# A graph network in four layers: edge weights moved to ScalarE and run counts cut in halves

## The chip, the cores and the metric

The kernel runs on one core of one Trainium2 chip. Times are device microseconds of one execution, from the start to the end of the program on that core. TensorE (PE) multiplies matrices; its weight loads (PEld) are shown apart, since they overlap its multiplications. VectorE (DVE) and ScalarE (ACT) work elementwise, GpSimd (POOL) issues the indirect gathers here, and SyncE (SP) issues plain DMAs.

## The reference

A graph of 3125 nodes with 256 features and 50,000 edges, sorted by their destination, goes through four layers. Each layer adds a graph network and a mixer to the nodes, and then a feed-forward part. The change touches layer 1's graph network only, two hypergraph convolutions in a row:

```python
def _hconv(x, src, dst, ew, w1, b1, w2, b2, g, b):
    h = jax.nn.relu(x @ w1 + b1)
    msg = ew[:, None] * h[src]
    agg = jax.ops.segment_sum(msg, dst, num_segments=x.shape[0])
    h = agg @ w2 + b2
    return jax.nn.relu(_bn(h, g, b))
...
h = _hconv(x, src, dst, hyperedge_weight, c1_w1, c1_b1, c1_w2, c1_b2, c1_g, c1_b)
h = jax.nn.relu(_bn(h, bn1_g, bn1_b))
h = _hconv(h, src, dst, hyperedge_weight, c2_w1, c2_b1, c2_w2, c2_b2, c2_g, c2_b)
h = _bn(h, bn2_g, bn2_b)
return jax.nn.relu(h + residual)
```

Layer 3's graph network has three convolutions over the same edges without weights. The kernel does them with a dense matrix that holds how many edges lead from each node to each other, and it builds that matrix while layer 1 runs.

## The kernel before

Nodes are padded to 25 blocks of 128 (`NB`). The edges are padded to 416 slots of 128 edges (`NS`), so that all edges of one slot have their destination in the same block. For each slot, `self.src` holds the 128 source rows, `self.dl` the destination within the block, `self.ew` the weight, and `self.blk` the block's number.

`gather_sum` is the loop over edges. It takes the slots in groups of four (`G`), 104 groups in all. For each slot of a group, POOL issues an indirect DMA (L531) that fetches 128 rows of 256 features from a table in DRAM into a part of the tile `msg`; the tile holds a group, and there are seven of them. DVE then makes, for each slot, a 128x128 one-hot `oh` of the destinations. With `weighted=True`, which layer 1 alone uses, the entry is the edge's weight in place of one, and each slot has its own `tensor_scalar` (L566); without it, `one_hot` makes four with one `tensor_tensor` (L538). TensorE multiplies each one-hot with the slot's messages into PSUM (`g`, L585; each fp32 multiplication is two instructions in the trace). DVE adds the four results of the group before to `agg` at the block's place, which it reads from `self.blk` at run time (L527, L544).

Layer 1 runs this loop twice, once per convolution. In `layer1`, `loop` hands `gather_sum` a generator `both`, from which it takes one step after each group. A step advances two other pieces of work: `mix1`, layer 1's mixer (59 steps, all within the first loop), and `more`, which is different work in each loop:

- In the first, `sorted_edges` sorts the edges of every run of 16 slots by source block into `self.rooms`, in 78 steps: eight of preparation, then ten rounds of seven. A round has one-hots of the source blocks (`ohk`), a scan, four products, and four one-hots `ohr` of 2048 columns (L2041).
- In the second, `counts` goes over the 40 runs (`NR`), two steps each. A run makes two one-hots for its 25 places, `ohs` and `ohd` (L2065, 128x3200 each, one buffer each). TensorE multiplies them place by place (L2078), four to a PSUM tile, after it has added the result of the run before, `last`, times `on` where the run goes on in the same block (L2076). ACT copies the PSUM tiles to `T` as bf16 (L2080; two buffers). Then DVE adds an identity to one block of `T` (L2088), ACT looks for counts too large to be exact (`junk`, L2091), and SP writes `T` to `self.counted` in DRAM (L2092).

The columns' numbers 0 to 127 lie in SBUF as `self.cols`. Layer 1 has a PSUM tile `sums` of three parts: the first is the accumulator of `mix1` (shown as `acc`), the second a copy of `self.cols`, the third the same plus one. `sorted_edges` and `counts` read the second and third.

The program states waits by the tiles that instructions read and write. A scheduler puts the instructions of each engine into an order when the program is built, so that instructions of the loop, the mixer and `more` are mixed on every engine; on the chip each engine keeps that order. Each gather waits for the matmuls that read its `msg` tile seven groups before.

Of the kernel before, what the change touches and what calls it, by code (L numbers as in the profile page):

```python
# [9 lines left out]
F32 = mybir.dt.float32  # L10
BF16 = mybir.dt.bfloat16
# [8 lines left out]
P = 128  # L20
# [10 lines left out]
G = 4  # L31
# [18 lines left out]
def bc(ap, shape):  # L50

    idx, full = [], []
    own = list(ap.shape)
    for n in shape:
        if n is None:
            idx.append(slice(None))
            full.append(own.pop(0))
        else:
            idx.append(None)
            full.append(n)  # L60
    assert not own
    return ap[tuple(idx)].to_broadcast(full)


class Net:
# [466 lines left out]
            out=out, out_offset=None, in_=table,  # L532
            in_offset=bass.IndirectOffsetOnAxis(ap=self.src[:, t:t + 1], axis=0))

    def one_hot(self, pool, g):

        oh = pool.tile([P, G, P], F32, name="oh")
        self.nc.vector.tensor_tensor(oh, bc(self.dl[:, g * G:(g + 1) * G], [None, None, P]),  # L538
                                     bc(self.cols, [None, G, None]), ALU.is_equal)
        return oh  # L540

    def add_to(self, agg, t, q, w):
# [4 lines left out]
        for j in range(G):  # L547
            self.add_to(agg, g * G + j, q[j], agg.shape[2])

    def gather_sum(self, pool, ps, table, w, agg, weighted=False, steps=None):  # L550

        nc = self.nc
        sums = {}
        n = 1024 // w
        for g in range(NS // G):
            msg = []
            for j in range(G):
                if j % n == 0:
                    m = pool.tile([P, n, w], F32, name="msg", bufs=7)
                self.gather(m[:, j % n, :], table, g * G + j)  # L560
                msg.append(m[:, j % n, :])
            if weighted:
                oh = pool.tile([P, G, P], F32, name="oh", bufs=3)
                for j in range(G):
                    t = g * G + j
                    nc.vector.tensor_scalar(oh[:, j, :], self.cols, self.dl[:, t:t + 1], self.ew[:, t:t + 1],  # L566
                                            op0=ALU.is_equal, op1=ALU.mult)
            else:
                oh = self.one_hot(pool, g)
            if g:  # L570
                self.add_group(agg, g - 1, sums.pop(g - 1))
            sums[g] = self.sum_group(ps, oh, msg, w)
            if steps is not None:
                next(steps, None)
        self.add_group(agg, g, sums.pop(g))
# [1089 lines left out]
    def layer1(self):  # L1665
        nc, tc = self.nc, self.tc
        self.norm_x()
        with self.pool("rooms", 1) as c, self.pool("gnn", 1) as gw, self.pool("gnn2", 2) as gp, \
                self.pool("mix", 1) as mw, self.pool("mix2", 2) as mp, \
                self.pool("ps1", 3, PSUM) as ps, ExitStack() as own:  # L1670
            pool = Pools(gw, gp, CONV_ONE)

            sums = ps.tile([P, 3, P], F32, name="acc0", bufs=1)
            nc.scalar.copy(sums[:, 1, :], self.cols)
            nc.vector.tensor_scalar(sums[:, 2, :], self.cols, 1.0, None, op0=ALU.add)
            steps = self.mix1(mw, mp, ps, sums[:, 0, :])

            def loop(tab, agg, more):
                def both():
                    for _ in range(NS // G):  # L1680
                        next(steps, None)
                        next(more, None)
                        yield

                self.gather_sum(pool, ps, tab, D, agg, weighted=True, steps=both())
                for _ in more:
                    pass


            self.rooms = c.tile([P, NR, 2 * NB], BF16, name="rooms")  # L1690
            self.run_blk = c.tile([1, NR], I32, name="run_blk")
            self.goes_on, self.begins = (c.tile([P, NR], F32, name=n) for n in ("goes_on", "begins"))

            self.unfit = c.tile([P, 3], F32, name="unfit")

            tab, agg, *rest = self.conv_head(pool, ps, 1, self.xT)
            with self.pool("sort", 1, side="right") as bp:
                with ExitStack() as inner:
                    loop(tab, agg, self.sorted_edges(bp, ps, inner, sums[:, 1, :]))
            with self.pool("res", 1, side="right") as hp:  # L1700
                hT = hp.tile([P, 2, NP], F32, name="hT")
                self.conv_tail(pool, ps, agg, *rest, hT)
                sc, sh = self.batch_norm(pool, hT, self.plain(gw, "L1_gnn_bn1_g"), self.plain(gw, "L1_gnn_bn1_b"), "bn")
                self.relu_of(hT, sc, sh)
                tab, agg, *rest = self.conv_head(pool, ps, 2, hT)
            with self.pool("count", 1, side="right") as bp:
                loop(tab, agg, self.counts(bp, ps, sums[:, 1:, :]))
            hp = own.enter_context(self.pool("res", 1, side="right"))
            hT = hp.tile([P, 2, NP], F32, name="hT")
            self.conv_tail(pool, ps, agg, *rest, hT)  # L1710
            for _ in steps:
                pass
            sc, sh = self.batch_norm(pool, hT, self.plain(gw, "L1_gnn_bn2_g"), self.plain(gw, "L1_gnn_bn2_b"), "bn")
            for s, n in SUPER:
                for k in range(2):
                    h = hT[:, k, s:s + n]
                    nc.vector.scalar_tensor_tensor(h, h, sc[:, k:k + 1], self.xT[:, k, s:s + n], op0=ALU.mult,
                                                   op1=ALU.add)
                    nc.scalar.activation(h, h, AF.Relu, bias=sh[:, k:k + 1])
                for t in range(s // P, (s + n) // P):  # L1720
                    q = ps.tile([P, 512], F32, name="mm")[:, :D]
                    for k in range(2):
                        nc.tensor.transpose(q[:, k * P:(k + 1) * P], hT[:, k, t * P:(t + 1) * P], self.ident)
                    self.add_x(t, q)
# [326 lines left out]
    def counts(self, p, ps, cols):  # L2051
# [6 lines left out]
        over = p.tile([P, NR, 2], F32, name="over")  # L2058
        nc.vector.memset(over, 0.0)
        last = None  # L2060
        for u in range(NR):
            oh = []
            for k, name in enumerate(("ohs", "ohd")):
                t = p.tile([P, NB, P], BF16, name=name)
                nc.vector.tensor_tensor(t, bc(self.rooms[:, u, k * NB:(k + 1) * NB], [None, None, P]),  # L2065
                                        bc(cols[:, 1 - k, :], [None, NB, None]), ALU.is_equal)
                oh.append(t)
            on = p.tile([P, P], BF16, name="on", bufs=2)
            nc.scalar.mul(on, ident, self.goes_on[:, u:u + 1])
            yield  # L2070
            T = p.tile([P, NB, P], BF16, name="T", bufs=2)
            for k0 in range(0, NB, 4):
                n = min(4, NB - k0)
                q = ps.tile([P, 512], F32, name="mm")[:, :n * P]
                if last is not None:
                    nc.tensor.matmul(q, on, last[:, k0:k0 + n, :], start=True, stop=False)  # L2076
                for k in range(n):
                    nc.tensor.matmul(q[:, k * P:(k + 1) * P], oh[0][:, k0 + k, :], oh[1][:, k0 + k, :],  # L2078
                                     start=last is None, stop=last is None or k == n - 1)
                nc.scalar.copy(T[:, k0:k0 + n, :], q.rearrange("p (k d) -> p k d", d=P))  # L2080
                if k0 == 12:
                    yield

            Tf = T.rearrange("p k d -> p (k d)")
            r = nc.values_load(self.run_blk[0:1, u:u + 1], engines=(ET.DVE, ET.SP), min_val=0, max_val=NB - 1,
                               skip_runtime_bounds_check_because=IN_RANGE)
            own = Tf[:, bass.ds(r * P, P)]
            nc.vector.scalar_tensor_tensor(own, ident, self.begins[:, u:u + 1], own, op0=ALU.mult, op1=ALU.add)  # L2088
            for i, k0, k1 in ((0, 0, 13), (1, 13, NB)):
                junk = p.tile([P, 13 * P], BF16, name="junk")[:, :(k1 - k0) * P]  # L2090
                nc.scalar.activation(junk, Tf[:, k0 * P:k1 * P], AF.Relu, bias=full, accum_out=over[:, u, i:i + 1])  # L2091
            nc.sync.dma_start(self.counted[bass.ds(r * P, P), :], Tf)  # L2092
            last = T
        nc.vector.tensor_reduce(self.unfit[:, 1:2], over.rearrange("p u i -> p (u i)"), axis=AX.X, op=ALU.max)
        nc.vector.tensor_scalar(self.unfit[:, 1:2], self.unfit[:, 1:2], 0.0, None, op0=ALU.is_gt)
        one = p.tile([P, 1], F32, name="one")
# [313 lines left out]
```

## Time and profile before

| | |
|---|---|
| median of 3 runs | 6230.42 us (6222.06 to 6235.17) |
| the profiled execution | 6871.84 us, span 6870.1 us |
| instructions | 81944 |
| busy: PE, PEld, DVE | 4752.5, 3363.4, 3279.0 us |
| busy: ACT, POOL | 1573.9, 2383.8 us |
| granted TensorE clock, mean | 0.825 |
| loop 1, first gather to last add | 683 us |
| loop 2, first gather to last add | 808 us |
| layer 1's gathers (L531) | 832, 820.0 us busy, 986 ns each |
| weighted one-hots (L566) | 832, median 340 ns each |
| adds to `agg` (L544), all layers | 1664, 697.1 us busy |
| `ohs`, `ohd` (L2065) | 40 each, medians 3486 and 3479 ns |
| copies to `T` (L2080) | 280, median 586 ns |

The profile is of one execution, and that execution was 641 us longer than the median of the runs without it. Busy time of an engine is the sum of its instructions' durations; on DVE and ACT neighbours overlap a little, so that they can start closer together than they last. "Idle before, with a releaser" names the instruction whose end let a waiting one start. "Remote" and "another core or an unknown queue" are stalls for which the profile found no releaser.

### The profile page before, as it was taken

How to read it: one execution, taken by the hardware profiler on the slowest of the kernel's cores; microseconds unless marked ns; L12 is line 12 of the kernel's file. 1: busy time of each engine (PE TensorE's matmuls, PEld its weight loads, DVE VectorE, ACT ScalarE, POOL GpSimd, SP SyncE). 2: the span in 40 equal slices, each digit the busy share in tenths (PEclk: the TensorE clock that was granted, in tenths of full speed). 3: DMA queues.
4: the chain of work that ended last, by engine and by line, in shares of the span. 5: the costliest groups of instructions: out<-in, count | busy, mean ns of one | idle time of the engine just before them, and what ended most of it. 6: DMA issues, size and time to landing. Idle time of an engine off the chain costs nothing.

```text
span 6870.1 us, 81944 instructions
## 1 busy us (share of the span) xinstructions
PE 4752.5 (69%) x25310; PEld 3363.4 (49%) x25310; DVE 3279.0 (48%) x8628; ACT 1573.9 (23%) x4113; POOL 2383.8 (35%) x2340
## 2 busy tenths in 40 slices
PE   2375776396575556555577756777169999997797
PEld 1012344284454434433366313444046788786696
DVE  5146676634687537775534346667533200113222
ACT  1012223322100034442222112221124311101222
POOL 1605776321665534445231625665110000001211
PEclk9677888598787777777688877888589999997898
DMA  3362333264222223333155322333111232123454
GB/s 106 85 179 66 107 107 102 83 199 118 86 84 74 71 76 116 116 109 102 53 167 173 90 79 83 102 107 94 37 55 62 72 135 87 58 78 113 171 175 160
DMA packets 385094, 710.59 MB, mean 103 GB/s; under 512 B 100817, under 2 KB 223256, under 8 KB 384652
## 3 DMA queue, kind: packets, MB, share of 16 engines
q1 hardware_dynamic: 266431, 425.79, 20.0%
q0 software_dynamic: 108064, 269.63, 13.6%
q10 hardware_dynamic: 10157, 9.80, 0.4%
q8 instruction: 213, 3.49, 0.2%
q14 instruction: 229, 1.88, 0.1%
HBM read 571.51 MB, written 133.47 MB: 103 GB/s over the span
## 4 chain that ended last, share of the span: by engine, by line
PE 46%; issue 17%; DVE 15%; another core or an unknown queue 8%; DMA 5%; POOL 4%; ACT 3%; DVEq 2%; ACTq 1%; SPq 0%; POOLq 0%
PE dn L2134 12%; PE mm L465 6%; PE g L862 5%; PE g L585 3%; DVE agg L544 3%; PE y L1507 3%; PE h L1494 2%; DVE ohd L2065 2%; PE q L657 1%; PE q L666 1%; DMA terms<-outr 1%; PE mm L502 1%; DVEq L527 1%; PE mm L2194 1%
## 5 line engine op out<-in xcount | busy, mean ns | idle before, releaser
L531 POOL DMA_INDIRECT msg<-L_gnn_c_tab,src x832 | 820.0, 986 | 857.4 <-PE g L585 236.2
L531 POOL DMA_INDIRECT msg<-L_gnn_htab,src x832 | 893.7, 1074 | 588.6 <-issue 225.2
L544 DVE TENSOR_TENSOR agg<-agg,g 128x256 f32 (+2 forms) x1664 | 697.1, 419 | 588.6 <-remote 283.5
L2134 PEld LDWEIGHTS <-a 128*128 128x128 bf16 x7500 | 735.0, 98 | 118.1 <-issue 30.2
L862 PE MATMUL g<-msg,oh 128*128 128x261 f32 (+1 forms) x1664 | 591.8, 463 | 248.7 <-DVE agg L544 114.2
L585 PE MATMUL g<-msg,oh 128*128 128x256 f32 x1664 | 565.9, 489 | 229.0 <-DVE oh L566 138.7
L862 PEld LDWEIGHTS g<-msg,oh 128*128 128x128 f32 x1664 | 324.0, 218 | 510.3 <-issue 213.7
L585 PEld LDWEIGHTS g<-msg,oh 128*128 128x128 f32 x1664 | 387.7, 249 | 345.9 <-DVE oh L566 156.4
L1494 PE MATMUL h<-xe,w 128*128 128x128 f32 x3584 | 435.6, 278 | 7.3 <-DMA w<-in_L_ffn_W 7.3
L2134 PE MATMUL dn<-ha,a 128*128 128x256 bf16 x3750 | 426.2, 274 | 9.3 <-ACT ha L2119 7.8
L1511 POOL DMA_INDIRECT back<-y,toi x168 | 163.2, 971 | 773.4 <-DVE y L1510 537.9
L1507 PE MATMUL y<-w,hT 128*128 x1792 | 431.2, 388 | 0.0
L1494 PEld LDWEIGHTS h<-xe,w 128*128 128x128 f32 x3584 | 421.1, 194 | 8.7 <-issue 8.3
L2134 PE MATMUL dn<-hb,a 128*128 128x256 bf16 x3750 | 413.6, 273 | 0.0
L1498 ACT ACTIVATE hT<-h,br 128x128 f32<-128x128 f32 x896 | 256.3, 369 | 661.0 <-issue 572.7
L1418 POOL IOTA sl<- 1x56 f32 x3 | 0.5, 171 | 1123.7 <-PE dn L2134 1023.8
L1507 PEld LDWEIGHTS y<-w,hT 128*128 128x128 f32 x1792 | 326.5, 190 | 57.0
L1510 DVE COPY y<-y 128x256 f32<-128x256 f32 x168 | 71.2, 424 | 574.6 <-PE y L1507 574.4
L819 ACT COPY stage<-dm 128x24 bf16 (+1 forms) x832 | 182.7, 221 | 578.9 <-PE pd L825 193.5
L657 PE MATMUL q<-ohl,t 128*104 128x512 bf16 (+1 forms) x702 | 204.1, 423 | 126.3 <-issue 69.7
L1389 POOL DMA_INDIRECT sent<-xs,ids x150 | 154.8, 1032 | 355.9 <-DVE run L1368 189.2
L531 POOL DMA_INDIRECT ase<-tab,src x208 | 219.1, 1054 | 151.7 <-PE q L657 85.7
(724 smaller groups left out, 7619.8 us busy)
## 6 DMA issues: line engine op xcount, KB each, us to landing
a<-counted SPq DMA_DIRECT2D x100, 800.0 KB
w<-in_L_ffn_W SPq DMA_DIRECT2D x128, 512.0 KB
w<-in_L_ffn_W SPq DMA_DIRECT2D x64, 1024.0 KB
counted<-T SPq DMA_DIRECT2D x40, 800.0 KB
dr<-dl_rows SPq DMA_DIRECT2D x104, 256.0 KB
sent<-zeros SPq DMA_DIRECT2D x25, 1040.0 KB
xr<-sent SPq DMA_DIRECT2D x168, 130.0 KB
lw<-lo_rows SPq DMA_DIRECT2D x78, 256.0 KB
```

Source lines behind the costliest of these rows:

```text
L465: nc.tensor.matmul(q, xT[:, k, t * P:(t + 1) * P], w[:, k, cols], start=(k == 0 and bias is None), stop=(k == nk - 1))
L531: self.nc.gpsimd.indirect_dma_start(out=out, out_offset=None, in_=table, in_offset=bass.IndirectOffsetOnAxis(ap=self.src[:, t:t + 1], axis=0))
L544: self.nc.vector.tensor_tensor(at, at, q, ALU.add)
L585: self.nc.tensor.matmul(r, oh[:, j, :], msg[j], start=True, stop=True)
L657: nc.tensor.matmul(q[:M], t3[:, k, i, :], oh[:, k, :], start=((k, i) == mm[0]), stop=((k, i) == mm[-1]))
L819: nc.scalar.copy(rows[:, j, :], dmf[:, bass.ds(at, 6 * H)])
L862: nc.tensor.matmul(q, oh[:, j, :], msg[:, j, :], start=True, stop=True)
L1494: nc.tensor.matmul(q[:, i, :], d["w1"][:, k, c * P:(c + 1) * P], d["xe"][:, k, :], start=(k == 0), stop=(k == 1))
L1498: nc.scalar.activation(hT[:, c, :], q[:, i, :], act, bias=d["br"][:, c:c + 1])
L1507: nc.tensor.matmul(q, d["hT"][:, c, :], w2f[:, bass.ds(e * (nh * D) + c * D, D)], start=False, stop=(c == nh - 1))
L1511: s = nc.gpsimd.indirect_dma_start(out=self.back, out_offset=bass.IndirectOffsetOnAxis(ap=d["to"][:, 0:1], axis=0), in_=y, in_offset=None)
L2134: nc.tensor.matmul(q, a[:, k, :], h[:, k, i, :], start=(k == 0 and i == 0), stop=(k == NB - 1 and i == 2))
```

## The change

In `gather_sum` the weighted one-hots go. ACT now multiplies each slot's messages, in place, with the weights of its edges, and `one_hot` makes the group's four one-hots with one `tensor_tensor` that reads the column numbers from PSUM. In `loop`, `more` is no longer advanced after each of the first groups until it ends, but after 80 of the 104 groups, spread evenly. In `counts`, a run's one-hots come in two parts of 12 and 13 places with two buffers each, a step ends after each part, and what finishes a run (the identity, the look for large counts and the write to DRAM, now in `finish`) comes after the first one-hots of the next run.

```diff
--- before.py
+++ after.py
@@ -532,11 +532,11 @@
             out=out, out_offset=None, in_=table,
             in_offset=bass.IndirectOffsetOnAxis(ap=self.src[:, t:t + 1], axis=0))
 
-    def one_hot(self, pool, g):
-
-        oh = pool.tile([P, G, P], F32, name="oh")
+    def one_hot(self, pool, g, cols=None, **more):
+
+        oh = pool.tile([P, G, P], F32, name="oh", **more)
         self.nc.vector.tensor_tensor(oh, bc(self.dl[:, g * G:(g + 1) * G], [None, None, P]),
-                                     bc(self.cols, [None, G, None]), ALU.is_equal)
+                                     bc(self.cols if cols is None else cols, [None, G, None]), ALU.is_equal)
         return oh
 
     def add_to(self, agg, t, q, w):
@@ -547,7 +547,7 @@
         for j in range(G):
             self.add_to(agg, g * G + j, q[j], agg.shape[2])
 
-    def gather_sum(self, pool, ps, table, w, agg, weighted=False, steps=None):
+    def gather_sum(self, pool, ps, table, w, agg, weighted=False, steps=None, cols=None):
 
         nc = self.nc
         sums = {}
@@ -560,11 +560,9 @@
                 self.gather(m[:, j % n, :], table, g * G + j)
                 msg.append(m[:, j % n, :])
             if weighted:
-                oh = pool.tile([P, G, P], F32, name="oh", bufs=3)
                 for j in range(G):
-                    t = g * G + j
-                    nc.vector.tensor_scalar(oh[:, j, :], self.cols, self.dl[:, t:t + 1], self.ew[:, t:t + 1],
-                                            op0=ALU.is_equal, op1=ALU.mult)
+                    nc.scalar.mul(msg[j], msg[j], self.ew[:, g * G + j:g * G + j + 1])
+                oh = self.one_hot(pool, g, cols, bufs=3)
             else:
                 oh = self.one_hot(pool, g)
             if g:
@@ -1677,12 +1675,14 @@
 
             def loop(tab, agg, more):
                 def both():
-                    for _ in range(NS // G):
+                    for g in range(NS // G):
                         next(steps, None)
-                        next(more, None)
+
+                        if (g + 1) * 80 // (NS // G) > g * 80 // (NS // G):
+                            next(more, None)
                         yield
 
-                self.gather_sum(pool, ps, tab, D, agg, weighted=True, steps=both())
+                self.gather_sum(pool, ps, tab, D, agg, weighted=True, steps=both(), cols=sums[:, 1, :])
                 for _ in more:
                     pass
 
@@ -2058,28 +2058,9 @@
         over = p.tile([P, NR, 2], F32, name="over")
         nc.vector.memset(over, 0.0)
         last = None
-        for u in range(NR):
-            oh = []
-            for k, name in enumerate(("ohs", "ohd")):
-                t = p.tile([P, NB, P], BF16, name=name)
-                nc.vector.tensor_tensor(t, bc(self.rooms[:, u, k * NB:(k + 1) * NB], [None, None, P]),
-                                        bc(cols[:, 1 - k, :], [None, NB, None]), ALU.is_equal)
-                oh.append(t)
-            on = p.tile([P, P], BF16, name="on", bufs=2)
-            nc.scalar.mul(on, ident, self.goes_on[:, u:u + 1])
-            yield
-            T = p.tile([P, NB, P], BF16, name="T", bufs=2)
-            for k0 in range(0, NB, 4):
-                n = min(4, NB - k0)
-                q = ps.tile([P, 512], F32, name="mm")[:, :n * P]
-                if last is not None:
-                    nc.tensor.matmul(q, on, last[:, k0:k0 + n, :], start=True, stop=False)
-                for k in range(n):
-                    nc.tensor.matmul(q[:, k * P:(k + 1) * P], oh[0][:, k0 + k, :], oh[1][:, k0 + k, :],
-                                     start=last is None, stop=last is None or k == n - 1)
-                nc.scalar.copy(T[:, k0:k0 + n, :], q.rearrange("p (k d) -> p k d", d=P))
-                if k0 == 12:
-                    yield
+        H = 12
+
+        def finish(u, T):
 
             Tf = T.rearrange("p k d -> p (k d)")
             r = nc.values_load(self.run_blk[0:1, u:u + 1], engines=(ET.DVE, ET.SP), min_val=0, max_val=NB - 1,
@@ -2090,7 +2071,32 @@
                 junk = p.tile([P, 13 * P], BF16, name="junk")[:, :(k1 - k0) * P]
                 nc.scalar.activation(junk, Tf[:, k0 * P:k1 * P], AF.Relu, bias=full, accum_out=over[:, u, i:i + 1])
             nc.sync.dma_start(self.counted[bass.ds(r * P, P), :], Tf)
+
+        for u in range(NR):
+            T = p.tile([P, NB, P], BF16, name="T", bufs=2)
+            on = p.tile([P, P], BF16, name="on", bufs=2)
+            nc.scalar.mul(on, ident, self.goes_on[:, u:u + 1])
+            for h0, h1 in ((0, H), (H, NB)):
+                oh = []
+                for k, name in enumerate(("ohs", "ohd")):
+                    t = p.tile([P, NB - H, P], BF16, name=name, bufs=2)[:, :h1 - h0]
+                    nc.vector.tensor_tensor(t, bc(self.rooms[:, u, k * NB + h0:k * NB + h1], [None, None, P]),
+                                            bc(cols[:, 1 - k, :], [None, h1 - h0, None]), ALU.is_equal)
+                    oh.append(t)
+                if last is not None and h0 == 0:
+                    finish(u - 1, last)
+                for k0 in range(h0, h1, 4):
+                    n = min(4, h1 - k0)
+                    q = ps.tile([P, 512], F32, name="mm")[:, :n * P]
+                    if last is not None:
+                        nc.tensor.matmul(q, on, last[:, k0:k0 + n, :], start=True, stop=False)
+                    for k in range(n):
+                        nc.tensor.matmul(q[:, k * P:(k + 1) * P], oh[0][:, k0 - h0 + k, :], oh[1][:, k0 - h0 + k, :],
+                                         start=last is None, stop=last is None or k == n - 1)
+                    nc.scalar.copy(T[:, k0:k0 + n, :], q.rearrange("p (k d) -> p k d", d=P))
+                yield
             last = T
+        finish(NR - 1, last)
         nc.vector.tensor_reduce(self.unfit[:, 1:2], over.rearrange("p u i -> p (u i)"), axis=AX.X, op=ALU.max)
         nc.vector.tensor_scalar(self.unfit[:, 1:2], self.unfit[:, 1:2], 0.0, None, op0=ALU.is_gt)
         one = p.tile([P, 1], F32, name="one")
```

## The prediction

> **What bounds the kernel now.** The change touches only layer 1's two edge loops (one per hypergraph convolution), so I first read the busy time of the engines in the two stretches from the first gather to the last add of each loop: PE, PEld, DVE, ACT and POOL busy, granted clock, DMA share, GB/s.
>
> ```profile
> 1706.00:2389.00 683.00, 422.96 (x2115) 314.73 (x2113) 466.26 (x1046) 38.98 (x145) 425.94 (x416) 0.77 0.28 81
> 2492.00:3300.00 808.00, 446.47 (x2107) 313.81 (x2107) 536.87 (x940) 290.59 (x477) 394.04 (x416) 0.71 0.34 109
> ```
>
> Loop 1 takes 683 us, loop 2 takes 808 us. No engine is full: DVE is busy 68% and 66%, ACT 6% and 36%. So the loops are bound by waits. Both issue 416 gathers, and those set a floor: in the timeline POOL starts one every 1.25 us when nothing stops it (0.95 us and 0.30 us of issue), 5.0 us for a group of four, 520 us for a loop.
>
> Next the chain of waits in order of time, and the timeline, within loop 2:
>
> ```profile
> 2846.65 3.41 DVE ohd L2065
> ...
> 2853.36 2.68 PE g L585 x8
> ...
> 2862.86 3.41 DVE ohd L2065
> ...
> 2869.56 3.10 PE g L585 x8
> ```
>
> ```profile
> 2859.11 3.49 DVE L2065 TENSOR_TENSOR ohs<-rooms,acc 128x3200 bf16<-128x3200 bf16 x1 [4.34 <-PE g L585]
> ...
> 2862.52 0.35 DVE L2088 SCALAR_TENSOR_TENSOR T<-identb,begins,T 128x128 bf16 x1
> 2862.78 3.48 DVE L2065 TENSOR_TENSOR ohd<-rooms,acc 128x3200 bf16<-128x3200 bf16 x1
> ...
> 2862.90 1.68 ACT L2091 ACTIVATE junk<-T,full 128x1664 bf16<-128x1664 bf16 x1 [2.78 <-DVE T L2088]
> ...
> 2866.31 0.58 PE L2078 MATMUL mm<-ohd,ohs 128*128 128x128 bf16 x4 [1.96 <-DVE ohd L2065]
> ...
> 2868.13 0.97 POOL L531 DMA_INDIRECT msg<-L_gnn_c_tab,src  x1 [6.49 <-PE g L585]
> ...
> 2875.38 3.49 DVE L2065 TENSOR_TENSOR ohs<-rooms,acc 128x3200 bf16<-128x3200 bf16 x1 [4.41 <-PE g L585]
> ```
>
> A run of `counts` repeats every 16.26 us (2859.11 to 2875.38) and is a circle through one buffer: DVE makes both one-hots (7.1 us with the small `T` write), TensorE may then start (wait of 1.96 us), and `ohs` and `ohd` have one buffer each, so DVE may not write the next `ohs` before the matmuls have read this one: 4.3 to 4.4 us of idle DVE per run. Two groups of gathers go with each run, so POOL, which needs 10.0 us for them, waits 6.5 us. From the first `ohs` (2487.5) to the last `ohd` (3173.6) there are 40 runs in 686 us; 34.3 us of that is one stall put down to an unknown queue, so 16.3 us a run. Then 24 groups are left without runs, and they take 126 us.
>
> The groups of instructions of loop 2 by shape give the prices, and the timeline of its last groups shows DVE alone:
>
> ```profile
> L531 POOL DMA_INDIRECT msg<-L_gnn_c_tab,src x416 | 394.1, 947 | 515.5 <-PE g L585 166.8 <-DMA L_gnn_c_tab<-hb 119.2 <-issue 110.5
> L585 PE MATMUL g<-msg,oh 128*128 128x256 f32 x832 | 286.4, 495 | 66.2 <-DVE oh L566 31.9 <-DVE agg L544 21.1 <-DMA msg<-L_gnn_c_tab,src 8.2
> L544 DVE TENSOR_TENSOR agg<-agg,g 128x256 f32 x416 | 172.9, 416 | 100.1 <-remote 59.5 <-PE g L585 14.6 <-issue 10.0
> ```
>
> ```profile
> 3292.77 0.98 DVE L544 TENSOR_TENSOR agg<-agg,g 128x256 f32 x2 [0.19 <-PE g L585]
> 3293.67 1.11 DVE L566 TENSOR_SCALAR oh<-cols,dl,ew 128x128 f32<-128x128 f32 x4
> ...
> 3294.70 0.87 DVE L544 TENSOR_TENSOR agg<-agg,g 128x256 f32 x2
> ```
>
> Four adds and four one-hots take 2.98 us of DVE. Two adds next to each other are some 0.5 us apart, since each waits for the one before; with another instruction between, the timeline has 0.33 us for the add and 0.26 us for a one-hot.
>
> **What the Trainium skill says.** "VectorE: DVE Perf Modes", The perf-mode tier table: an fp32 `tensor_tensor` runs at one element a cycle, an fp32 `tensor_scalar` from SBUF at two. The trace agrees: 683 ns for the 512-wide one-hot of layers 0 and 2 (L538), 340 ns for 128 with L566. "GPSIMD Engine Reference", 1. Specifications: POOL's SBUF interface is shared with DVE and contended by two-port DVE modes or two SBUF inputs. The trace agrees: a gather beside the scan at 1932.98 takes 4.14 us against 0.95. The new one-hot reads its columns from PSUM, so I charge POOL nothing. "ScalarE: Activation LUTs", What ACT_TABLE_LOAD costs: a per-partition pointer adds about 93 ns, and neighbours overlap by as much; 457 and 474 ns for the 128x256 multiplies by a pointer (`vv`, `z`) fit. "TensorE: Matmul & The Clock Gate", What's actually happening: idleness halves the clock. The trace has 0.71 granted in loop 2, and eight `g` matmuls between 1.99 and 3.8 us.
>
> **The change part by part**, per run of loop 2, which now gets 104/40 = 2.6 groups.
> - *Spread*: 80 steps over 104 groups, not over the first 80. No instruction changes. The 24 bare groups go, their work moves into the runs.
> - *Weights on ScalarE*: adds 416 multiplies per loop. No trace line has SBUF to SBUF fp32 of that width; 0.41 us (`on`, half as wide) and 0.474 us bound it, I take 0.46, less some 0.09 of overlap. ACT per run: seven copies 3.8, two `junk` with their reads 3.6, `on` 0.4, 10.4 multiplies 4.8, less 18 overlaps of 0.1: 10.8 us. Each multiply waits for its own gather; behind it in ACT's order stand the `T` copies and `junk`, and TensorE waits for it.
> - *One-hot of four*: 0.60 us apart in place of 4 x 0.26. But adds now have fewer instructions between them: in the changed program's order 104 of 399 adds in the runs follow an add directly. So DVE gains about nothing here.
> - *Halves, double-buffered*: 3.47 us per pair become 1.80 and 1.67 (1664 and 1536 wide at the same slope), 6.94 per run. What goes is the circle: `ohs` of the next run no longer waits for TensorE.
> - *`T` write and its DMA* now stand behind the first one-hots of the next run. The `counted` DMA on SP's queue is 0.84 MB and had landed long before the next (SP waited 2.75 us for it, then 14.1 us for DVE), so I cost that at nothing; at worst it is 3 us per run.
>
> DVE per run: adds 10.4 x 0.33 plus 2.6 x 0.2 for neighbours = 4.0; one-hots 2.6 x 0.60 = 1.6; halves 6.9; `T` 0.3: 12.8 us. POOL: 10.4 x 1.25 = 13.0. ACT 10.8. TensorE at full clock 2.6 x 2.0 for the groups and 7 x 0.4 for the counts = 8.0. The late one next is thus POOL with DVE close behind. Two engines this near to full, in order, do not both run without a wait; I choose 14.0 (0.4 us of DVE waits per group, as in the last groups now), with 13.0 and 15.5 as ends. Loop 2: 40 x 14.0 + 8 = 568, plus the 58 us of unknown stalls that it has now (34 and 24 at its end) = 626. Saved: 182.
>
> Loop 1: gathers 520, plus 32 for those slowed beside two-input DVE work (mean 1024 against 947 ns, x 416), plus some 100 of unknown stalls = 652 at the floor. Its DVE work for 9.1 groups is 40 us against 45.5 of POOL. The one-hots now read the PSUM tile into which `mix1` accumulates, a wait that the `ohr` one-hots have already (19.7 us in ten waits); for 25 groups I take 6 us, 0 to 50 as bounds. Saved: 25 (-20 to 31).
>
> Sum: 207. The profiled execution has 6871.8 us (span 6870.1), which becomes 6665. The median of the runs shown is 641 us shorter; stalls that only the profiled run may have are left in on both sides, so the saving carries over: 6230 - 207, about **6025**.
>
> **Rivals.** *ACT's order is the bound* (15%): copies of `T` stand behind multiplies that wait for gathers. ACT now waits 209 us for the count matmuls, which speaks for it; 36% busy against it. At 15.5 us a run and no gain in loop 1, 182 - 60 = 122 are saved: 6108. *The circle stays* (10%), through `T` (DVE, TensorE, ACT, DVE) instead of `ohs`: 16.3 plus 0.6 groups of TensorE (1.2) = 17.5, loop 2 = 766, saved 42: 6188. For it: TensorE waits 137 us for `T`. Against it: half of its wait is for DVE's one-hots. *Slower* (9%): the gathers' lead is lost, and each group runs gather (2.8 us from issue to use at 2492), four multiplies (1.6), matmuls (2.0), adds in a row, some 7.5 us. The two loops without stalls are now 1333 us for 208 groups, so it decides from 6.4 us a group; 7.5 gives 6230 + 227 = 6457. Against it: seven message buffers let POOL lead by 35 us. *At the floor in both* (15%): 13.0 a run, 5977.
>
> **How the numbers follow.** The likeliest case (48%, 14.0 a run) gives 6025, its own range 5965 to 6085. Rivals faster than before: 15, 15 and 10%. No change 3%, slower 9%; 0.2% (12 us) is about what a measurement can tell from no change. Range 5945 to 6195 takes in all four faster cases but for their far ends, and leaves out the slower and equal ones, 12%, and some 5% beyond the floor.
>
> **What would show it.** After: no `ohs` wait on `g`; runs 13 to 15 us apart; POOL's wait for `g` near zero in loop 2; the bare groups gone; ACT over 75% busy there. Wrong would be: runs 16 us apart or more; multiplies or `T` copies as the releaser of most TensorE waits; gathers slowed beside the new one-hot.

## The result, and the profile after

The changed kernel takes 6261.0 us (median of 5 runs, 6259.46 to 6267.86), the kernel before 6230.42 us (5 runs): a ratio of 1.0052, 95% interval 1.0037 to 1.0066. It is slower by half a per cent, where 3.3% faster was predicted. A second comparison, among the experiments, gave 1.0058 (1.0045 to 1.0072).

The profiled execution took 6267.86 us, span 6266.1, the longest of the five and 0.1% above their median, so this profile can stand for it. First the busy time by stretch, from the first gather to the last add of each loop; columns as in the prediction (length, then PE, PEld, DVE, ACT and POOL busy, granted clock, DMA share, GB/s).

```profile
1509.00:2124.00 615.00, 422.82 (x2107) 314.27 (x2108) 432.72 (x736) 236.49 (x557) 425.37 (x416) 0.78 0.30 89
2227.00:2872.00 645.00, 403.53 (x2107) 273.91 (x2104) 502.42 (x717) 455.26 (x893) 394.62 (x416) 0.86 0.42 136
```

Loop 1 takes 615 us and loop 2 645 us, 1260 together. Beside the 683 and 808 of the profile before this looks like a gain of 231 us, yet the time did not fall. The two profiles can't be set against each other: parts that the change doesn't touch are also shorter, such as layer 0's edge loop with 838 us (188 to 1026) against 1030 (189 to 1219). The experiments below supply a profile of before that can be compared.

What waits in loop 2 now, from its waits (waiting instruction, releaser: total us, times, longest):

```profile
ACT msg L564 <- DMA msg<-L_gnn_c_tab,src: 170.4, 200, 3.3
PE mm L2092 <- ACT T L2096: 146.0, 78, 7.6
...
POOL msg L531 <- ACT msg L564: 49.4, 29, 6.9
POOL msg L531 <- ACT T L2096: 45.6, 16, 3.7
DVE T L2069 <- ACT T L2096: 43.5, 24, 5.7
```

The wait of `ohs` for TensorE is gone, as the change intends. In its place ACT's multiplies (L564) wait 170 us for gathers to land, TensorE waits 146 us for ACT's copies of `T`, and POOL waits 95 us for ACT. In loop 1 the same wait of the multiplies is larger still:

```profile
ACT msg L564 <- DMA msg<-L_gnn_c_tab,src: 328.9, 366, 5.1
```

The groups of instructions in loop 2, by shape (count | busy us, mean ns | idle before, releasers):

```profile
L531 POOL DMA_INDIRECT msg<-L_gnn_c_tab,src x416 | 394.6, 949 | 343.1 <-PE mm L2094 132.5 <-issue 112.2 <-ACT msg L564 49.4
L583 PE MATMUL g<-msg,oh 128*128 128x256 f32 x832 | 268.5, 454 | 63.2 <-DVE agg L544 57.3 <-ACT msg L564 4.7
L564 ACT ACTIVATE msg<-msg,ew 128x256 f32<-128x256 f32 x416 | 199.7, 508 | 172.4 <-DMA msg<-L_gnn_c_tab,src 170.4
L544 DVE TENSOR_TENSOR agg<-agg,g 128x256 f32 x413 | 172.1, 417 | 37.1 <-DVE agg L544 13.1 <-DVE oh L538 4.9 <-DVE T L2069 4.6
...
L538 DVE TENSOR_TENSOR oh<-dl,acc 128x512 f32<-128x512 f32 x102 | 69.7, 683 | 62.0 <-PE g L583 61.8
```

Gathers and adds have their old prices (949 and 417 ns). A multiply takes 508 ns. DVE waits 62 us before its new one-hot for TensorE's `g`.

How these waits hang together shows in the timeline of loop 2:

```profile
2584.52 0.95 POOL L531 DMA_INDIRECT msg<-L_gnn_c_tab,src  x1 [0.30 <-issue]
2584.74 0.51 ACT L564 ACTIVATE msg<-msg,ew 128x256 f32<-128x256 f32 x1 [0.72 <-DMA msg<-L_gnn_c_tab,src]
...
2586.76 0.51 ACT L564 ACTIVATE msg<-msg,ew 128x256 f32<-128x256 f32 x1 [1.51 <-DMA msg<-L_gnn_c_tab,src]
...
2587.17 1.71 ACT L2096 CAST T<-mm 128x512 bf16<-128x512 f32 x4
...
2587.79 0.26 PE L2092 MATMUL mm<-T,on 128*128 128x128 bf16 x1 [4.21 <-ACT T L2096]
...
2587.95 3.72 PE L583 MATMUL g<-msg,oh 128*128 128x256 f32 x8
...
2592.42 0.95 POOL L531 DMA_INDIRECT msg<-L_gnn_c_tab,src  x1 [3.19 <-ACT msg L564]
```

ACT waits 0.72 and 1.51 us for gathers to land, and four copies of `T` stand behind those multiplies in its order. TensorE has stood 4.21 us for these copies, and behind the matmul that waits stand the products of a group (eight instructions, four slots) whose gathers were started some six groups earlier (counted below). A message tile comes free when such products have read it. POOL then stands still for 3.19 us, until 2592.42. The view names a multiply as what released it, but the products above end at the same moment as that multiply (2591.67 us, the multiply 2591.66), so either may have been it. So it looks as if a transfer that is needed only six groups later holds up work of now, and that work the next transfers. Whether that is what costs the time is for the experiments.

### The profile page after: what moved, and what is told of

The parts are those of the page before. It is cut to its first block, busy times and chain, and to the rows that moved or that the text cites. A ratio compares the mean times of both kernels' runs of the same rounds, so it can differ in the third digit from the quotient of the medians.

```text
span 6266.1 us, 81335 instructions
## 1 busy us (share of the span) xinstructions
PE 4640.2 (74%) x25310; PEld 3305.3 (53%) x25310; DVE 3211.1 (51%) x8087; ACT 1936.3 (31%) x4942; POOL 2390.8 (38%) x2340
## 5 line engine op out<-in xcount | busy, mean ns | idle before, releaser
L860 PE MATMUL g<-msg,oh 128*128 128x261 f32 (+1 forms) x1664 | 573.8, 454 | 189.8 <-DVE agg L544 175.2
L583 PE MATMUL g<-msg,oh 128*128 128x256 f32 x1664 | 547.8, 465 | 118.6 <-DVE agg L544 81.9
L564 ACT ACTIVATE msg<-msg,ew 128x256 f32<-128x256 f32 x832 | 407.6, 508 | 507.8 <-DMA msg<-L_gnn_c_tab,src 499.3
L860 PEld LDWEIGHTS g<-msg,oh 128*128 128x128 f32 x1664 | 317.3, 213 | 428.6 <-DVE agg L544 320.7
L583 PEld LDWEIGHTS g<-msg,oh 128*128 128x128 f32 x1664 | 357.7, 231 | 289.5 <-DVE agg L544 140.0
L849 DVE TENSOR_TENSOR msg<-msg,alpha 128x1024 f32<-128x1024 f32 x208 | 254.3, 1223 | 129.3 <-DMA msg<-L_gnn_htab,src 115.9
```

The costliest lines, as they stand in the source:

```text
L564: nc.scalar.mul(msg[j], msg[j], self.ew[:, g * G + j:g * G + j + 1])
L583: self.nc.tensor.matmul(r, oh[:, j, :], msg[j], start=True, stop=True)
L849: nc.vector.tensor_tensor(mh, mh, bc(al_, [None, None, None, C]), ALU.mult)
L860: nc.tensor.matmul(q, oh[:, j, :], msg[:, j, :], start=True, stop=True)
```

## The experiments

Theory A is that ScalarE's multiplies, in their order with the copies of `T`, cost what the rest gains. Its rivals are B, the circle of `counts` or its halves, C, DVE's time, and the even spread. D, E and F came up later and say what it is about the multiplies. (The "Rival D" in what was expected of `e4_front` is the even spread, not the later Theory D.) A ratio is the time of a run to that of the kernel before on the same chip; below 1 is faster.

**Undoing one part at a time, first on a chip with stalls.** These four ran on a chip on which the kernel before takes 6895.94 us (median of 43 runs, 6849.54 to 6925.73), not 6230 us. Its profile there has the stalls without a releaser that the profile in the prediction has, and nearly its loops (690 and 810 us), so that profile was probably of such a chip; which one it was is not on record.

`e1_before`: before, unchanged.

> The kernel before, unchanged, for a second profile. Its first profiled execution was 641 us longer than its median, and some 340 us of that lay in layers 0 and 2, which the change does not touch; the changed kernel's profiled execution is within 5 us of its median. Theory 'slowed profile': a second profile comes out near 6230 us with few remote stalls; the two loops together then take about 1228 us (1259 in the changed kernel less the 31 us between the medians), not 1491, and a run of counts well under 16.26 us. Rival 'profiling always costs this kernel 600 us': again about 6870 us, the loops 1491 us.

Measured 6887.51 us (18 runs, ratio 0.9997, 0.9977 to 1.0016). The profile of 6862.5 us is thus what an execution on that chip is like. Neither theory of the expectation holds: a second profile is as long as the first, but it is not the profiler that makes it long.

`e2_noact`: the changed kernel with weights back in the one-hots:

```diff
+                oh = pool.tile([P, G, P], F32, name="oh", bufs=3)
                 for j in range(G):
-                    nc.scalar.mul(msg[j], msg[j], self.ew[:, g * G + j:g * G + j + 1])
-                oh = self.one_hot(pool, g, cols, bufs=3)
+                    t = g * G + j
+                    nc.vector.tensor_scalar(oh[:, j, :], self.cols, self.dl[:, t:t + 1], self.ew[:, t:t + 1],
+                                            op0=ALU.is_equal, op1=ALU.mult)
```

> The changed kernel with the weights back in VectorE's one-hots; halves and even spread stay. Theory A, 'ScalarE's order': the T copies stand behind multiplies that wait for gathers (TensorE waited 146 us for T copies in loop 2), so without the multiplies a run falls from 16.0 to about 13.5 us, loop 2 from 645 to some 550 us, and the time to about 6150 us. Rival B, 'the circle through T stays': a run stays at 16 us, the time within 15 us of 6261. Rival C, 'VectorE was bound': more VectorE instructions, slower than 6261 by 20 us or more.

Measured 6751.19 us, ratio 0.9788 (0.9753 to 0.9824).

`e3_whole`: the changed kernel with `counts` of before, its one-hots whole and single-buffered.

> The changed kernel with counts as before: whole one-hots in one buffer, finish of a run at its end; the multiplies on ScalarE and the even spread stay. Theory A: the single buffer comes on top of ScalarE's order, so slower than 6261, about 6330 us. Rival B: counts in halves is what cost time, so faster, about 6200 us.

Measured 6859.02 us, ratio 0.9946 (0.9928 to 0.9963).

`e4_front`: the changed kernel with a step of `more` after each of the first groups again:

```diff
-                        if (g + 1) * 80 // (NS // G) > g * 80 // (NS // G):
-                            next(more, None)
+                        next(more, None)
```

> The changed kernel with the steps of the sort and the counts in the first 80 groups again. Theory A: with 2.0 in place of 2.6 groups a run has fewer multiplies and the bare groups come back at 5 us each: runs of about 14 us (560 us) and 120 us of bare groups, slower by 20 to 40 us, about 6290 us. Rival D, 'spreading costs': the mixed groups are where the time is lost, so faster than 6261 by 20 us or more.

Measured 6836.16 us, ratio 0.9918 (0.9887 to 0.9949). Without the multiplies the gain is the largest, so they are the suspect. The changed kernel was not run on this chip, so no part has a price from these four, and the times in their expectations, which start from 6261 us, can't be held against them.

**The parts again, on chips without the stalls.** The rest ran on chips where before takes 6242 to 6252 us.

`g_after`: the changed kernel itself.

> The changed kernel itself, beside the kernel before on the same chip. Theory A (ScalarE's multiplies cost what the rest of the change gains, wherever it runs): where before takes about 6230 us, 6261 us again, ratio 1.005; where before takes about 6890 us, the stalls come on top of the loops of both and it gains no more than the runs that undo a part (0.979 to 0.995): about 0.99. Rival (the profile of before was of an execution with stalls in its gathers, and the change hides such stalls): ratio 0.97 or less, about 6690 us, where before takes 6890.

Measured 6286.66 us, ratio 1.0058 (1.0045 to 1.0072).

`g_noact`: the edit of `e2_noact`.

> The changed kernel with the weights back in VectorE's one-hots (no multiply on ScalarE); halves and spread stay. Theory A: faster than before everywhere: ratio 0.975 to 0.985, about 6110 us where before takes 6230; and below the changed kernel by 1 to 2%. Rival (it is faster only where the stalls are): same as before within 0.3% on a chip without them.

Measured 6171.45 us, ratio 0.9871 (0.9856 to 0.9886).

`g_halves`: the kernel before with the new `counts` and `finish` alone.

> The kernel before with the runs' one-hots in two double-buffered parts alone. Theory A: the circle through the single buffers is gone, so part of the gain of the run without multiplies, ratio 0.985 to 0.995. Rival B (the circle was not what bounded the loop): within 0.2% of before.

Measured 6176.89 us, ratio 0.9879 (0.9864 to 0.9894).

`g_act`: the kernel before with the multiplies and the one-hot of four alone (the edit of `e2_noact` the other way round).

> The kernel before with the weights put on the messages by ScalarE and the one-hot of four slots from PSUM alone; counts and their order as before. Theory A: slower than before, ratio 1.005 to 1.02 (ScalarE's in-order multiplies hold the copies of the counts). Rival C (VectorE's time bounds the loops, and the saving of some 1.0 us a group is worth something): ratio below 0.99.

Measured 6433.41 us, ratio 1.029 (1.0276 to 1.0305), worse than expected. `e3_whole` is `g_act` with the even spread, and was 0.5% faster than before on the chip with stalls. Whether the spread or the stalls make that difference, no run tells. The stretches of loop 1 and loop 2 of `g_halves`, `g_noact` and `g_act`, in this order:

```profile
1515.00:2077.00 562.00, 437.84 (x2107) 301.49 (x2105) 462.24 (x1041) 39.04 (x142) 429.33 (x416) 0.81 0.34 98
2180.00:2775.00 595.00, 403.66 (x2101) 281.65 (x2100) 540.80 (x1024) 271.20 (x477) 394.62 (x416) 0.84 0.47 148
```

```profile
1519.00:2083.00 564.00, 424.26 (x2105) 300.76 (x2105) 460.62 (x1041) 37.06 (x141) 433.43 (x416) 0.83 0.34 98
2187.00:2773.00 586.00, 399.79 (x2093) 284.63 (x2093) 538.46 (x1016) 266.48 (x470) 393.88 (x416) 0.84 0.47 148
```

```profile
1516.00:2150.00 634.00, 455.13 (x2108) 320.15 (x2106) 430.81 (x731) 238.54 (x558) 428.60 (x416) 0.77 0.30 87
2253.00:3042.00 789.00, 475.38 (x2107) 327.72 (x2107) 508.50 (x646) 469.74 (x893) 394.24 (x416) 0.71 0.35 111
```

The halves are worth 75 us (6251.92 less 6176.89). The even spread on top of them gives 5 us more, within the intervals; what it is worth together with the multiplies was not measured. The two loops with multiplies take 1423 us in `g_act`, with DVE 60 us less busy than in `g_noact`: what ACT took over, DVE no longer does, and the time went up all the same.

**What before does without the stalls.**

`h_before`: before, unchanged.

> The kernel before, for its loops in an execution of the shorter kind. If halves alone saved 75 us in loop 2 (594 us there) and changed nothing in loop 1 (561 us), then loop 1 takes about 561 us and loop 2 about 669 us, 1230 us together, against 1491 us in the profile that the prediction read; the runs of counts are then about 13.5 to 14.5 us apart, not 16.3. Rival: loop 2 is near 800 us here too, and the difference lies in the other layers.

Measured 6247.7 us, one run. Its two loops, and the waits of `ohs` in loop 2:

```profile
1508.00:2071.00 563.00, 438.13 (x2106) 303.89 (x2104) 461.78 (x1036) 38.92 (x142) 429.26 (x416) 0.81 0.34 98
2176.00:2845.00 669.00, 429.17 (x2107) 300.15 (x2107) 537.38 (x943) 286.00 (x477) 393.42 (x416) 0.75 0.42 131
```

```profile
DVE ohs L2065 <- PE mm L2078: 54.5, 29, 4.5
```

The loops take 563 and 669 us, 1232 together and not 1491; the runs of `counts` are a median of 13.66 us apart and a mean of 14.60, not 16.26. (So the rival in the expectation falls.) The circle through the single buffers costs 54.5 us in the whole loop, some 1.4 us a run, where the timeline in the prediction showed 4.3.

**Where a multiply stands in ScalarE's order.** This can be counted in the traces. When a copy of `T` starts in loop 2 of `g_after`, ScalarE has begun the multiplies of 5.75 groups (median of 279 copies) for which TensorE has not begun the products. And a multiply starts there 3.0 us after its gather was started (median of 416), with only two later gathers started by then. So the multiplies follow right behind the gathers, and the copies behind the multiplies. In place a multiply needs no new buffer, which leaves the scheduler free to put it as early as its gather. The next runs move the multiplies or leave them out.

`h_late52`: the multiply writes a tile of its own, of which there are two, and there are five message tiles in layer 1:

```diff
-                    m = pool.tile([P, n, w], F32, name="msg", bufs=7)
+                    m = pool.tile([P, n, w], F32, name="msg", bufs=5 if weighted else 7)
...
+                wm = pool.tile([P, G, w], F32, name="wm", bufs=2)
                 for j in range(G):
-                    nc.scalar.mul(msg[j], msg[j], self.ew[:, g * G + j:g * G + j + 1])
+                    nc.scalar.mul(wm[:, j, :], msg[j], self.ew[:, g * G + j:g * G + j + 1])
+                    msg[j] = wm[:, j, :]
```

> The changed kernel with the multiplies writing a tile of their own, of which there are two, and five message tiles in place of seven. A multiply can then stand no more than two groups ahead of TensorE's use of it in ScalarE's order; in the changed kernel it stands six groups ahead, right where its gather lands, with the copies of T behind it. Same multiplies, same buffers in all. Theory D (it is the multiplies' place in ScalarE's order, behind the newest gather, that costs): ratio to before 0.975 to 0.988, about 6130 us where before takes 6250, and ScalarE's waits for gathers in loop 2 fall from 172 us to under 50. Theory A (ScalarE's own time, or the step more between landing and use, wherever it stands): 1.000 to 1.006, about 6280 us.

Measured 6140.69 us, ratio 0.9833 (0.982 to 0.9847): the 2.2% come back, with every multiply still there. Its loops:

```profile
1505.00:2069.00 564.00, 419.24 (x2108) 311.27 (x2109) 431.28 (x736) 210.36 (x557) 426.22 (x416) 0.81 0.34 98
2172.00:2742.00 570.00, 401.50 (x2099) 267.62 (x2099) 499.60 (x724) 440.07 (x892) 393.63 (x416) 0.87 0.49 154
```

ACT is as busy in loop 2 as in the changed kernel, 440 us against 455, and the loop is 75 us shorter. So it is not ACT's own time. What TensorE waits for in loop 2 shows the difference, 17.2 us for copies of `T` where it was 146.0:

```profile
PE mm L2094 <- ACT T L2098: 17.2, 23, 4.0
```

`h_late61`: the same with six message tiles and one multiplied.

> The same with one tile for multiplied messages and six message tiles: multiplies at most one group ahead of TensorE. Theory D: the waits for gathers are gone as well, but TensorE now waits for the multiplies of each group, so between the kernel with two and the changed kernel: ratio 0.980 to 1.000. Theory A: 1.006 or more.

Measured 6138.8 us, ratio 0.9835 (0.9822 to 0.9849). One tile is enough. TensorE's weight loads do wait longer for multiplies, as Theory D said (140.3 us over both loops, 62.2 in `h_late52`), but the time is the same.

`h_nomul`: the multiplies left out, so that messages go in without their weights.

```diff
-                for j in range(G):
-                    nc.scalar.mul(msg[j], msg[j], self.ew[:, g * G + j:g * G + j + 1])
```

> The changed kernel with the multiplies left out, so that the messages are not weighted: the one-hots of four slots, halves and spread stay. Theory D and A alike: the 115 us between the changed kernel and the one with weights in VectorE's one-hots come back, and some of the 64 us of VectorE time that the one-hot of four saves in both loops: ratio 0.975 to 0.988. Rival (the one-hot that reads PSUM, not the multiply, costs the time): above 1.000.

Measured 6147.49 us, ratio 0.9847 (0.9833 to 0.986). With no multiply at all it is not faster than with multiplies well placed: so placed, they cost nothing that can be measured, and in place they cost 2.1% (1.0058 less 0.9847, each against before on its own chip). The new one-hot and the even spread are still in this run, so neither is what costs.

`k_early25` and `k_early34`: `h_late52` with two and five, and with three and four tiles (`bufs=2` and `bufs=5`, `bufs=3` and `bufs=4`).

> The kernel with a tile of its own for the multiplied messages, now five of these and two message tiles: seven in all and the same multiplies, but the multiplies may stand up to five groups ahead of TensorE in ScalarE's order, right behind the newest gather, as in the changed kernel. Theory D (the place in ScalarE's order): the gain of the kernel with five and two is lost, ratio 0.998 to 1.010, ScalarE waits over 120 us for gathers in loop 2. Theory E (what helped was that a message tile is free for the next gather once it is multiplied, not once TensorE has read it): that holds here too, ratio 0.980 to 0.988.

> The same with three message tiles and four multiplied ones, the multiplies up to four groups ahead. Theory D: between the kernel with two and five (about 1.00) and that with five and two (0.983), nearer the former: 0.988 to 1.003. Theory E: 0.980 to 0.988.

Measured 6187.45 us, ratio 0.9903 (0.9887 to 0.9919), and 6161.71 us, ratio 0.9868 (0.9851 to 0.9884). Both are faster than Theory D said; the second lies in Theory E's range, the first in neither.

`k_msg4`: the changed kernel with `bufs=4` for the message tiles of layer 1.

> The changed kernel, multiplies in place, with four message tiles in place of seven in layer 1. A multiply can stand three groups ahead of TensorE, but still right behind the newest gather, since gathers have lost the same three tiles. Theory D: it is the distance from the gather, not from TensorE, that counts, so no gain: ratio 1.003 to 1.02. Theory F (the distance ahead of TensorE itself, six groups, is what harms): 0.985 to 0.998.

Measured 6276.59 us, ratio 1.0051 (1.0037 to 1.0065). Half as many groups ahead of TensorE (copies of `T` start 2.88 groups ahead, not 5.75) bring no gain, against Theory F. The edit also shortens the lead of the gathers over TensorE, to a median of 10 slots in loop 1 from 19 in `g_after`, which could have eaten up a gain. But `h_late61` has a lead of 7 slots there and runs loop 1 in 555 us, against 607, so such a lead is enough for loop 1. Theory F falls there; for loop 2 this one run speaks against it. Of the other two neither is right as stated. Theory D left out that a message tile which is free once it is multiplied lets the next gathers run ahead of the multiplies; Theory E gives no reason for two and five to do worse than five and two. What orders the runs is how far gathers are ahead of the multiplies. In place a multiply starts 3.0 to 3.6 us after its gather; with a tile of their own for the multiplies, gathers can be ahead by as many groups as there are message tiles. The table has this time, taken from the traces, beside the waits. These are the multiplies' own groups, over both loops, in `g_after`, `k_early25` and `h_late52`, each with what it waited for (us, times):

```profile
L564 ACT ACTIVATE msg<-msg,ew x832: 491/508/540, 1518.4 to 2856.5; 128x256 f32<-128x256 f32 x167
...
  DMA msg<-L_gnn_c_tab,src: 504.6, 567
```

```profile
L565 ACT ACTIVATE wm<-msg,ew x832: 491/508/552, 1521.0 to 2767.9; 128x256 f32<-128x256 f32 x167
...
  DMA msg<-L_gnn_c_tab,src: 233.7, 280
  PE g L585: 144.9, 90
```

```profile
L565 ACT ACTIVATE wm<-msg,ew x832: 491/494/547, 1507.5 to 2730.5; 128x256 f32<-128x256 f32 x167
...
  PE g L585: 250.7, 109
...
  DMA msg<-L_gnn_c_tab,src: 47.5, 55
```

| run | message tiles, multiplied tiles | start of a gather to start of its multiply, loop 2, median us | multiplies wait for gathers, us | both loops, us | ratio to before |
|---|---|---|---|---|---|
| `g_after` | 7, in place | 3.0 | 504.6 | 1266 | 1.0058 |
| `k_msg4` | 4, in place | 3.6 | 520.6 | 1265 | 1.0051 |
| `k_early25` | 2, 5 | 5.5 | 233.7 | 1171 | 0.9903 |
| `k_early34` | 3, 4 | 10.1 | 136.4 | 1144 | 0.9868 |
| `h_late52` | 5, 2 | 20.5 | 47.5 | 1134 | 0.9833 |
| `h_late61` | 6, 1 | 26.7 | 43.3 | 1129 | 0.9835 |

The loops get shorter as the wait for gathers does. The other wait grows from two and five to five and two, 144.9 to 250.7 us for TensorE's `g`, and does no harm. A likely reason is that ACT then waits for work that TensorE has ahead of it anyway, not for a transfer that POOL started a moment ago. That it is the wait for gathers, and not something else which goes with the number of tiles, rests on this series alone.

`h_late52` and `h_late61` beat both kernels, by 1.65 to 1.7% the one before.

## Why the prediction was wrong

The forecast of 207 us saved became 31 us lost, on chips without the stalls (loops of `h_before` 1232 us, of the changed kernel 1260 to 1266). The 238 us between them are four terms, each from loop lengths of one gather to the last add (`h_before` 670 and 564, `h_late52` 569 and 563, `g_after` 647 and 618, each read to the start of the last add and so within a microsecond of the stretches above).

- **"Stalls are left in on both sides, so the saving carries over": 81 us.** This step failed. Loop 2 was taken as 750 us without the stalls (808 less 58), and it is 669. The 58 us are stalls of the adds. In the waits of loop 2 in the same profile some of those of `ohs` have no releaser either, and the prediction counted them with the circle, which the change was to remove:

```profile
DVE agg L544 <- remote: 59.5, 7, 34.3
DVE ohs L2065 <- remote: 52.5, 13, 4.4
DVE ohs L2065 <- PE g L585: 52.0, 12, 4.4
```

  All waits of `ohs` come to 114.6 us there, 2.9 us a run and not 4.3, and to 54.5 us in `h_before`. Without these 52.5 us loop 2 would have been taken as 696 us. The other 27 us had no label: they lie in the distance of the runs, a median of 16.23 us there and of 13.66 in `h_before`, and why is open. The right step would have been to ask where the 641 us between profile and median lie, and to doubt every distance read there.
- **The sum of a run, 14.0 us: right, but for another kernel.** Loop 2 was to take 568 us without stalls, with runs 14.0 us apart. `h_late52` takes 569 us, mean 14.17. So near do DVE and POOL come to full when ACT doesn't hold them up. Of the 14.0 us, 13.0 were POOL's and 1.0 a choice, so that it agrees this well is in part luck.
- **"Each multiply waits for its own gather; behind it stand the `T` copies": 78 us in loop 2.** The prediction named this and then priced ACT by its busy time, 10.8 us a run, which left the waits for landing at nothing. This step failed too, and with loop 1 below it decides the sign: the same change with the multiplies moved saves 102 us (`h_late52`, 6140.69 against 6242.39). The runs came a mean of 16.1 us apart (`ohs` to `ohs`, median 14.2). `g_after` has 647 us against the 569 of `h_late52`.
- **Loop 1: 24 us of gain that isn't there, and 55 us of loss.** Predicted 25 us saved. With the multiplies well placed 564 us become 563, so loop 1 had nothing to give once its stalls were gone; in the changed kernel it takes 618. Its multiplies, for which the prediction set no loss but for the PSUM tile, wait 329 us for gathers. Behind them stand ACT's copies for the mixer and the sort: TensorE's multiplications wait 61 us for ACT in loop 1, and 18 us in `h_late52`.

Smaller terms: a multiply took 508 ns, not 460. The prediction found no line for fp32 of that width from SBUF to SBUF; the profile has one, a squaring with a pointer in another mixer, with nearly the price (`vv` and `z`, which it went by, read PSUM):

```profile
L1192 ACT ACTIVATE sq<-qk,s x25: 497/505/508, 4172.5 to 4523.6; 128x256 f32<-128x256 f32 x25
```

The new one-hots lowered DVE's busy time by 66 us over both loops (999 in `h_before`, 933 in `h_nomul`), where "about nothing" was expected; in time that is some 15 us, not clear of the noise (`g_noact` 0.9871, `h_nomul` 0.9847, whose intervals meet). The PSUM tile shared with `mix1` cost a DVE wait of 24.1 us in `g_after`, within the bounds of 0 to 50.

The rivals: *ACT's order is the bound* was the mechanism. Its price, 15.5 us a run and no gain in loop 1, was too low (a mean of 16.1, and a loss of 55 us), and it started from the same stalled loops. *The circle stays through `T`* is refuted by `g_halves`, which has that circle and gains 75 us. *Slower, the gathers' lead is lost* had the sign right and half the mechanism: gathers keep their lead over TensorE, but the multiplies follow them with none. Its point of decision, 6.4 us a group, was 5.9 without the stalls (1232 us for 208 groups); the changed kernel is at 6.1.

Of the signs that the prediction named: `ohs` no longer waits, the bare groups are gone, and POOL waits 0.8 us for `g`; but it waits 95 us for ACT instead. ACT is at 71% (455 of 645 us), not over 75%. Of its signs of error, runs 16 us apart are there (mean; the median is 14.2), and so are ACT's copies and multiplies as the releaser of most waits of TensorE's multiplications (152 of 240 us in loop 2); gathers are not slowed (949 ns).

## What to carry to other kernels

Here a step was put between a transfer and its consumer, on an engine that works in order and has other work. Since it wrote in place it could stand right behind the transfer, and the engine's other work stood behind it and waited for the landing. With one or two tiles of its own, and the rest of the buffers left to the transfers, the same step cost nothing that could be measured; with five of seven tiles of its own it still cost. So look at what such a step waits for and what stands behind it, not at how busy the engine is. And when the profiled execution is much longer than the median, first compare a stage that the change doesn't touch: here a saving read off the distances in such a profile did not carry over.

## What the runs showed of the hardware

The same kernel took 6230 to 6252 us (medians) on some chips and 6896 us on another, in all 43 runs there; its stalls have no releaser in the profile, and layer 0's edge loop, which the change leaves alone, has them as well as layer 1's (1031 us there, 832 us in `h_before`). What makes them was not found. An ACT multiply of 128x256 fp32 by a pointer took a median of 508 ns where ACT had been idle before it, in every run that has it, in place or into another tile. Without an idle before it, it took 493 ns in `h_late52` and `h_late61` and 502 to 507 ns in the others.
